# Denominators of the second attention layer: gathered into 32 rows per tile of tokens by four transfers, and one 128x4 product per block in place of four one-column products

## The chip, the cores and the metric

The kernel runs on one core of a Trainium2 chip. The metric is the device time of one execution in microseconds (us). Three runs of the kernel before the change took 3127.09, 3128.89 and 3130.44 us; the median is 3128.89 us.

## The reference, cut to what matters

Four images of 64x64 = 4096 tokens with 256 channels pass through two attention layers, one after the other. In each layer every token attends to all 4096 tokens of its image.

```
# layer 0
q, k, v = x @ Wq + bq, x @ Wk + bk, x @ Wv + bv        # 32, 32, 256 columns
x = gamma * softmax(q @ k.T) @ v + x
# layer 1
g, f, v = x @ Wg + bg, x @ Wf + bf, x @ Wh + bh        # 32, 32, 128 columns
x = x + softmax(g @ f.T) @ v @ Wo + bo
```

The softmax is computed without a maximum: the exponentials are summed unnormalised, the product with v is made from them, and the result is divided by the sum of the exponentials (the denominator) at the end. This case is about the denominators of layer 1.

## The kernel before, in words

**Blocks and steps.** An image takes 256 steps, 128 for each layer. In layer 1 the 4096 queries are cut into 8 blocks (j = 0 to 7) of 512, and a block takes 16 steps (i = 0 to 15), one for each 256 keys. A step makes the scores of 256 keys x 512 queries (L621, two steps ahead of their use), their exponentials p (L638, ScalarE), and the product of p with v (L713, TensorE). In the even steps ("split") p is cut into parts that TensorE multiplies faster: high (L631, ScalarE), low (L659) and d (L664, both VectorE). A block's accumulators are taken at step 15 (L770, L789) into o, 128 value columns x 512 queries.

**The sums.** The 16 tiles p of a block (128 partitions x 1024) have to be added up for the denominators. VectorE adds ten of them into p_sum (L678). The other six (steps 3, 5, 7, 9, 11 and 14; in the last image eight or seven) are added by transfers that accumulate into a tile p_sum_moved (L650 the first, L652 the others, here called moves). In images 0 to 2 all moves of a block go into one tile, so each waits until the one before has landed; in the last image they go into two tiles in turn, which a last transfer (L654) adds up. In the next block VectorE adds p_sum_moved to p_sum (add_moved, L778) and folds the two halves into the tile sums of 128 x 512 (fold, L782).

**The outputs.** `end_second` (L773) puts the rest of the work of a finished block into steps of the next block. `put(n, "a", ...)` runs it at the start of step n, and `put(n, "b", ...)` after the scores of that step were issued and before its products; "11b" below is the second place of step 11. For each of the four tiles t of 128 queries there are three stages: `multiply` (TensorE: o times Wo, L799, and then the column of denominators, L800: the 128x128 slice of sums as weights, a column of ones as the moving operand), `divide` (VectorE: reciprocal, L803) and `give` (ScalarE scales into y, L807, and a transfer adds y to the output in memory, L809). `multiply` stands at 9b, 10b, 12b and 13b of the next block (L67), at 5b to 8b in the kernel's last block (L68), and at 1b to 4b when the next block is the next image's first one of layer 0. The kernel's very last block is finished by code of its own (L836 to L875), which the change leaves as it is.

**What sets the order.** From step 8 on the order of instructions on each engine is the order in which the program issues them. Each engine works through its own list in that order and waits where an operand isn't there. All accumulating transfers are issued by POOL (GpSimd), together with the loads of q and k (L543) and, in layer 0, the residuals (L754, L1011). So a transfer that waits on POOL holds up every transfer behind it. When a sum on VectorE is issued is planned by two clocks (L1034, L1038, L1053) with a cost for each step, 0.63 us for each output among them.

**Buffers.** PSUM for side products (tag "side") has 2 buffers, shared by the outputs and the projections; the tiles "small" have 4; the tile p_sum_moved of images 0 to 2 and the tile sums have one each.

Of the kernel before, what the change touches and what calls it, by code (L numbers as in the profile page):

```python
# [50 lines left out]
F32 = mybir.dt.float32  # L51
F32R = mybir.dt.float32r
I32 = mybir.dt.int32
AF = mybir.ActivationFunctionType
ALU = mybir.AluOpType
AX = mybir.AxisListType

P = 128
QB = 512
QB0 = 256  # L60
NT = QB // P
S = 32
# [1 line left out]
EPS = 2.0**-12  # L64
UP = 2.0**12
AHEAD = 3
OUT_AT = (9, 10, 12, 13)  # L67
LAST_OUT_AT = (5, 6, 7, 8)  # L68
MOVED_AT = 1
KEEP, AHEAD_OF = 3, 1.0  # L70
Q_AHEAD = 6
# [179 lines left out]
def fast_path(ctx: ExitStack, tc: tile.TileContext, x, w0, w1, wo, bo, gamma, out, off):  # L251

    nc = tc.nc
    B, N, C = x.shape
# [8 lines left out]
    NI = (N // (G[0] * P), N // (G[1] * P))  # L263
# [8 lines left out]
    const = ctx.enter_context(tc.tile_pool(name="const", bufs=1))  # L272
    data = ctx.enter_context(tc.tile_pool(name="data", bufs=1))
    work = ctx.enter_context(tc.tile_pool(name="work", bufs=2))
    dram = ctx.enter_context(tc.tile_pool(name="dram", bufs=1, space=bass.MemoryType.DRAM))
# [25 lines left out]
    rows = {}  # L301
# [18 lines left out]
    nc.sync.dma_start(ident_dram, ident)  # L320
    ones = const.tile([P, 1], F32, name="ones")
    nc.vector.memset(ones, 1.0)

    inverse = const.tile([P, 2, B * N // P], F32, name="inverse")
    seen_v = const.tile([P, 2, B * NH], F32, name="seen_v")
# [29 lines left out]
    def side_psum(name):  # L355
        return ps_side.tile([P, QB], F32, tag="side", name=name)
# [3 lines left out]
    for j in range(NB):  # L360
        forms = {}
        for what, col in (("h", 1.0), ("l", 0.0), ("d", -EPS)):
            t = const.tile([P, NT, W], F32R, tag=f"v0{what}_{j}", name=f"v0{what}_{j}")
# [24 lines left out]
    q_t, moved_sums, first_p, later_sums, v_whole = {}, {}, [], [], {}  # L388
# [3 lines left out]
    def put(n, slot, *stages):  # L392
        todo.setdefault((n, slot), []).extend(stages)
# [167 lines left out]
    last_block = B * PER_IMAGE - NI[1]  # L561
# [30 lines left out]
    def small(name):  # L592
        return work.tile([P, C], F32, tag="small", bufs=4, name=name)
# [179 lines left out]
    def end_second(b, j, acc, p_sum, o, n_next):  # L773
        key = f"{b}_{j}"
        sums = [None]

        def add_moved():
            nc.vector.tensor_add(p_sum, p_sum, moved_sums[b, j, 0])  # L778

        def fold():  # L780
            sums[0] = work.tile([P, QB], F32, tag="sums", bufs=1, name=f"sums_{key}")
            nc.vector.tensor_add(sums[0].rearrange("p (a n) -> p a n", n=QB0), p_sum[:, :NS, :], p_sum[:, NS:, :])  # L782

        wait = j < NQ[1] - 1
        if not wait:
            while later_sums:
                later_sums.pop(0)[2]()
        for h in range(QB // QB0):
            nc.vector.tensor_add(o[h][:, :QB0], o[h][:, :QB0], acc[1][:, h * QB0 : (h + 1) * QB0])  # L789

        def output(t):
            tok = slice(t * P, (t + 1) * P)
            n = (b * N + j * QB) // P + t
            held = {}

            def multiply():
                held["ps"] = ps = side_psum(f"pso_{key}_{t}")
                part = o[t // NS][:, t % NS * P : (t % NS + 1) * P]
                nc.tensor.matmul(ps[:, :C], part, wo_sb, start=True, stop=True)  # L799
                nc.tensor.matmul(ps[:, C : C + 1], sums[0][:, tok], ones[:, :1], start=True, stop=True)  # L800

            def divide():
                nc.vector.reciprocal(inverse[:, 1, n : n + 1], held["ps"][:, C : C + 1])  # L803

            def give():
                y = small(f"y_{key}_{t}")
                nc.scalar.activation(y, held["ps"][:, :C], AF.Copy, scale=inverse[:, 1, n : n + 1])  # L807
                row = j * QB + t * P
                nc.gpsimd.dma_start(out[b, row : row + P, :], y, accum_op=ALU.add)  # L809

            return multiply, divide, give

        out_at = (1, 2, 3, 4) if not wait else OUT_AT if n_next < last_block else LAST_OUT_AT
        if wait:
            put(n_next + MOVED_AT, "b", lambda: later_sums.append((1.15, n_next + MOVED_AT + 3, add_moved, None)))
            put(n_next + MOVED_AT, "b", lambda: later_sums.append((0.6, n_next + MOVED_AT + 4, fold, f"p_sum_{b}_{j}")))
        else:
            put(n_next, "b", add_moved, fold)
        for t in range(NT):
            multiply, divide, give = output(t)  # L820
            at = n_next + out_at[t]
            put(at, "b", multiply)
            put(at + 1, "a", divide)
            put(at + 1, "b", give)

    ending = {}

# [64 lines left out]
    def put_all(n, at, stages):  # L892
        for where, stage in zip(at.split(), stages):
            put(n + int(where[:-1]), where[-1], stage)
# [64 lines left out]
    tensor_clock, vector_clock = 0.0, 0.0  # L959
# [27 lines left out]
    for n, s in enumerate(steps):  # L987
        now[0] = n
        b, l, j = s.b, s.l, s.j
# [24 lines left out]
        if ahead is not None and ahead.first:  # L1014
            k = (ahead.b, ahead.l, ahead.j * (QB0, QB)[ahead.l] // QB)
# [13 lines left out]
        if l == 0:  # L1029
            s.cut_both()  # L1030
            after.cut_low()
        else:
            cost = 1.9 if s.split else 2.2
            tensor_clock += cost + 1.7 * (b + 1 < B and s.i in (3, 7)) + 0.63 * (j > 0 and s.i in OUT_AT)  # L1034
            vector_clock = max(vector_clock, tensor_clock - cost)
            s.cut_both()
            after.cut_low()
            vector_clock += 1.15 * (s.split + after.split)  # L1038
            if n < len(steps) - 2:
                s.add_up(p_sum)  # L1040
        if l == 1:
# [11 lines left out]
            while later_sums and (later_sums[0][1] <= n or vector_clock + later_sums[0][0] <= tensor_clock + AHEAD_OF):  # L1053
                took, _, issue, _ = later_sums.pop(0)
# [12 lines left out]
            if n == len(steps) - 1:  # L1067
                last_outputs(acc, o)
            elif s.last:
                vector_clock += 0.8  # L1070
                end_second(b, j, acc, p_sum, o, n + 1)
# [23 lines left out]
def tile_two_attention_layers(tc: tile.TileContext, *args):  # L1095
    nc = tc.nc
    with tc.tile_pool(name="flag", bufs=1) as pool:
        off = pool.tile([1, 1], I32, name="off")
        fast_path(tc, *args, off)
        flag = nc.values_load(off[0:1, 0:1], min_val=0, max_val=4 * P, skip_runtime_bounds_check_because="a count")  # L1100
        with tc.If(flag < 1, preferred_fallthrough_block=False, label="in_range") as usual:
            pass
        with usual.Else():
            general_path(tc, *args)
# [40 lines left out]
```

## Time and profile before

| | us |
|---|---|
| median of three runs | 3128.89 |
| the profiled execution, its own time | 3129.13 |
| its span, first to last instruction | 3127.4 |
| TensorE (PE) busy | 3093.8 (99%) |
| VectorE (DVE) busy | 2732.4 (87%) |
| ScalarE (ACT) busy | 2203.5 (70%) |
| GpSimd (POOL) busy | 791.8 (25%) |
| L799, 248 matmuls with Wo, busy | 74.0 |
| L800, 248 one-column matmuls, busy | 34.4 |
| L803, 124 reciprocals, busy | 20.1 |

There are 31 blocks whose outputs go this way, so 124 outputs; each product in plain 32-bit floats is two matmuls with a weight load each, hence 248. The granted TensorE clock is 0.999 of full speed over the span. In the lines below, "L713 PE MATMUL acc<-p,v 128*128 128x512 f32 x4" is line, engine, operation, the tile written and those read, the shape, and how often; numbers in front are the start in us from the first instruction and the time until the end, and what stands in brackets is the idle time of the engine before it and what ended it. PE's ends are modelled and overlap the next start, so PE's pace is read from start to start.

### The profile page before, as it was taken

What the parts mean: (1) busy time and instruction counts of PE and PEld (TensorE: products, weight loads), DVE (VectorE), ACT (ScalarE), POOL (GpSimd) and SP (SyncE); (2) the same over time, 40 slices, a digit from 0 to 9 for tenths busy, and PEclk for the clock granted to TensorE, in tenths of its full rate; (3) what the DMA queues carried; (4) which work ended last, traced back from release to release, by engine and by line L of the source; (5) the groups of instructions that cost most, each with busy time, mean ns of one, the idle gap of its engine ahead of it and who ended that gap; (6) DMA issues with size and microseconds to landing.
All of it is one profiled execution on the core that took longest, in us unless ns stands there. A gap on an engine that the chain in (4) does not pass through costs nothing.

```text
span 3127.4 us, 55023 instructions
## 1 busy us (share of the span) xinstructions
PE 3093.8 (99%) x20052; PEld 2692.9 (86%) x20052; DVE 2732.4 (87%) x3328; ACT 2203.5 (70%) x2900; POOL 791.8 (25%) x1157
## 2 busy tenths in 40 slices
PE   8999999999999999999999999999999999999998
PEld 7999999666799999866679999986668999997665
DVE  6899889988888989998889988998888888888887
ACT  7767777777677777777767777677776666667775
POOL 4111113222411111422241111132234111123332
PEclk9999999999999999999999999999999999999999
DMA  4344455656644444656554444465565333337776
GB/s 124 75 89 89 84 96 115 127 115 118 125 85 84 93 89 87 128 121 118 117 110 92 84 89 90 88 133 115 115 128 97 63 70 72 60 76 158 154 154 140
DMA packets 441606, 325.86 MB, mean 104 GB/s; under 512 B 264466, under 2 KB 386196, under 8 KB 441332
## 3 DMA queue, kind: packets, MB, share of 16 engines
q0 software_dynamic: 112272, 196.49, 34.9%
q1 hardware_dynamic: 328148, 125.47, 16.8%
q8 instruction: 162, 2.65, 0.4%
q14 instruction: 112, 0.92, 0.1%
q10 hardware_dynamic: 912, 0.33, 0.1%
HBM read 128.45 MB, written 95.49 MB: 72 GB/s over the span
## 4 chain that ended last, share of the span: by engine, by line
PE 88%; DVE 3%; DMA 3%; issue 2%; ACT 2%; POOL 1%; SPq 0%; DVEq 0%; POOLq 0%; ACTq 0%
PE acc L689 23%; PE acc_pair L689 23%; PE acc L713 21%; PE st L621 14%; PE psv L497 4%; DMA p_sum_moved<-p 2%; PE psqk L446 2%; PE pso L799 1%; POOL k L543 1%; ACT p L638 0%; PE pso L800 0%; DVE d L664 0%; DVE low L659 0%; DVE p_sum L678 0%; ACT v0l L524 0%
## 5 line engine op out<-in xcount | busy, mean ns | idle before, releaser
L631 ACT ACTIVATE high<-st,down 128x1024 fp32r<-128x1024 f32 x651 | 728.2, 1119 | 686.9 <-PE st L621 609.1
L638 ACT ACTIVATE p<-st 128x1024 f32<-128x1024 f32 x1024 | 1028.9, 1021 | 20.3 <-DMA p_sum_moved<-p 9.3
L659 DVE TENSOR_TENSOR low<-p,high 128x1024 fp32r<-128x1024 f32 x565 | 690.7, 1223 | 144.4 <-ACT p L638 136.8
L664 DVE SCALAR_TENSOR_TENSOR d<-low,high 128x1024 fp32r<-128x1024 f32 x547 | 667.5, 1220 | 15.3 <-PE acc L713 0.7
L621 PE MATMUL st<-q,k 128*128 128x256 f32 (+1 forms) x3072 | 661.5, 323 | 0.6 <-DMA q<-qk_dram 0.5
L621 PEld LDWEIGHTS st<-q,k 128*128 128x128 f32 x3072 | 472.1, 189 | 57.5 <-issue 8.1
L713 PE MATMUL acc<-p,v 128*128 128x512 f32 (+1 forms) x1028 | 487.6, 596 | 0.8 <-DVE o L789 0.7
L689 PE MATMUL acc<-v0d,d 128*128 128x258 f32 x2048 | 336.5, 286 | 5.0 <-DVE d L664 4.7
L689 PE MATMUL acc<-v0h,high 128*128 128x258 f32 x2048 | 330.9, 284 | 1.2 <-ACT high L631 1.2
L689 PE MATMUL acc_pair<-v0l,low 128*128 128x256 f32 (+1 forms) x2048 | 329.9, 283 | 0.0
L689 PE MATMUL acc_pair<-v0h,high 128*128 128x258 f32 x2048 | 329.6, 283 | 0.0
L689 PE MATMUL acc<-v0l,low 128*128 128x256 f32 (+1 forms) x2048 | 328.1, 282 | 1.1 <-DVE low L659 0.8
L689 PE MATMUL acc_pair<-v0d,d 128*128 128x258 f32 x2048 | 328.8, 282 | 0.0
L754 POOL DMA_DIRECT2D out<-x x128 | 114.8, 897 | 839.3 <-DVE x L748 831.4
L713 PEld LDWEIGHTS acc<-p,v 128*128 128x128 f32 x1028 | 187.6, 189 | 143.1 <-issue 124.4
L678 DVE TENSOR_TENSOR p_sum<-p_sum,p 128x1024 f32<-128x1024 f32 x239 | 291.2, 1219 | 0.5
L689 PEld LDWEIGHTS acc<-v0d,d 128*128 128x128 f32 x2048 | 280.9, 189 | 7.8 <-DVE d L664 5.9
L689 PEld LDWEIGHTS acc<-v0h,high 128*128 128x128 f32 x2048 | 281.5, 189 | 3.0 <-ACT high L631 1.4
L689 PEld LDWEIGHTS acc<-v0l,low 128*128 128x128 f32 x2048 | 280.9, 189 | 2.6 <-DVE low L659 2.6
L689 PEld LDWEIGHTS acc_pair<-v0l,low 128*128 128x128 f32 x2048 | 282.4, 189 | 0.1
L689 PEld LDWEIGHTS acc_pair<-v0h,high 128*128 128x128 f32 x2048 | 281.9, 189 | 0.2 <-DVE o L733 0.2
L689 PEld LDWEIGHTS acc_pair<-v0d,d 128*128 128x128 f32 x2048 | 281.6, 189 | 0.0
(173 smaller groups left out, 4231.6 us busy)
## 6 DMA issues: line engine op xcount, KB each, us to landing
p_sum_moved<-p POOLq DMA_DIRECT2D x207, 512.0 KB, 5.0
x_res<-in_x SPq DMA_DIRECT2D x128, 128.0 KB, 3.2
qk_dram<-qk_parts SPq DMA_DIRECT2D x128, 128.0 KB, 2.2
x_res<-bias POOLq DMA_DIRECT2D x128, 128.0 KB, 4.1
out<-bias SPq DMA_DIRECT2D x128, 128.0 KB, 4.0
out<-x POOLq DMA_DIRECT2D x128, 128.0 KB, 3.1
q<-qk_dram POOLq DMA_DIRECT2D x252, 64.0 KB, 4.0
out<-y POOLq DMA_DIRECT2D x124, 128.0 KB, 3.5
```

Source lines behind the costliest of these rows:

```text
L446: nc.tensor.matmul(t["ps"], wqk[l][:, c, :], x_parts[key][n][:, c, :], start=(c == n == 0), stop=(c == NCC - 1 and n == 1),)
L497: nc.tensor.matmul(ps[:, n, :], xT[key][:, c, n * P : (n + 1) * P], wv[l][:, c, :], start=(c == 0), stop=(c == NCC - 1),)
L543: nc.gpsimd.dma_start(dst[n * D : (n + 1) * D, :], parts[h, which])
L621: nc.tensor.matmul(st[:, g, :], k_t[b, l, kt // NT][:, kt % NT * P : (kt % NT + 1) * P], q_t[b, l, j * n // QB][:, q0 : q0 + n], start=Tru ...
L631: nc.scalar.activation(self.high, s_flat, AF.Exp, bias=down)
L638: nc.scalar.activation(self.p, s_flat, AF.Exp)
L659: nc.vector.tensor_sub(self.low, self.p, self.high.bitcast(F32))
L664: nc.vector.scalar_tensor_tensor(self.d, self.low.bitcast(F32), -UP, self.high.bitcast(F32), ALU.mult, ALU.add)
L678: nc.vector.tensor_add(p_sum, other, self.p)
L689: nc.tensor.matmul(acc[2 * s + which][:, :width], p[:, g, s * P : (s + 1) * P], v0[self.i][v][:, g, :width], start=self.first and what != ...
L713: nc.tensor.matmul(acc[which].rearrange("p (a n) -> p a n", n=QB0)[:, cols, :], v_part[:, g, :], p[:, g * NS : (g + 1) * NS, :][:, cols, : ...
L754: nc.gpsimd.dma_start(out_rows(b, j, s), x_new, accum_op=ALU.add)
```

## The change

Before any output is multiplied, four transfers on POOL bring the tile sums into another shape. `fold_rows` adds its lower 64 partitions to its upper 64 inside SBUF. `store_rows` writes these 64 x 512 to memory. `gather(0)` reads the first 32 rows back into a tile rows of 128 x 128, whose partition is 32 t + r (t the tile of 128 queries, r the row); `gather(1)` adds the other 32 rows to it. Then one product, with rows as weights and a constant 128 x 4 matrix `quarters` (ones where the partition belongs to tile t) as moving operand, gives the denominators of all four tiles, as four columns in PSUM; it stands right behind the first output's product with Wo. One reciprocal of 128 x 4 replaces four of 128 x 1.

The places change too. The four transfers are put at 5a, 6b, 7b and 8b of the next block, or at 1a, 2a, 2b and 3b of the next image's first block. The outputs move to 11b, 12b, 14b and 15a, or 5a, 5b, 6b and 7a; the kernel's last block has no places of its own any more. The last dates for add_moved and fold are one step earlier, and the planner's cost for an output is 0.43 us at the last four steps. By the order of instructions of the changed kernel, POOL's list in a block of images 0 to 2 is: move of step 3, fold_rows, move of 5, store_rows, move of 7, gather(0), gather(1), move of 9, the four loads of q, move of 11, and so on; in the last image fold_rows stands behind the moves of 2 and 3, gather(0) ahead of the move of 8 and gather(1) behind it; in the kernel's last block gather(1) stands behind the L654 transfer.

```diff
-OUT_AT = (9, 10, 12, 13)
-LAST_OUT_AT = (5, 6, 7, 8)
+OUT_AT = "11b 12b 14b 15a"
+FIRST_OUT_AT = "5a 5b 6b 7a"
+GATHER_AT = "5a 6b 7b 8b"
+FIRST_GATHER_AT = "1a 2a 2b 3b"
...
+    quarters = const.tile([P, NT], F32, name="quarters")
+    nc.vector.memset(quarters, 0.0)
+    for t in range(NT):
+        nc.vector.memset(quarters[t * S : (t + 1) * S, t : t + 1], 1.0)
...
+        def fold_rows():
+            nc.gpsimd.dma_start(sums[0][: P // 2, :], sums[0][P // 2 :, :], accum_op=ALU.add)
+        def store_rows():
+            held["dram"] = dram.tile([P // 2, QB], F32, name=f"sums_dram_{key}")
+            nc.gpsimd.dma_start(held["dram"], sums[0][: P // 2, :])
+        def gather(k):
+            def issue():
+                if k == 0:
+                    held["rows"] = small(f"rows_{key}")[:, :P]
+                accumulate = dict(accum_op=ALU.add) if k else {}
+                part = held["dram"][k * S : (k + 1) * S, :].rearrange("r (t q) -> t r q", q=P)
+                nc.gpsimd.dma_start(held["rows"], part, **accumulate)
+            return issue
...
                 nc.tensor.matmul(ps[:, :C], part, wo_sb, start=True, stop=True)
-                nc.tensor.matmul(ps[:, C : C + 1], sums[0][:, tok], ones[:, :1], start=True, stop=True)
+                if t == 0:
+                    nc.tensor.matmul(ps[:, C : C + NT], held["rows"], quarters, start=True, stop=True)
             def divide():
-                nc.vector.reciprocal(inverse[:, 1, n : n + 1], held["ps"][:, C : C + 1])
+                if t == 0:
+                    nc.vector.reciprocal(inverse[:, 1, n : n + NT], held[t][:, C : C + NT])
...
-            put(n_next + MOVED_AT, "b", lambda: later_sums.append((1.15, n_next + MOVED_AT + 3, add_moved, None)))
-            put(n_next + MOVED_AT, "b", lambda: later_sums.append((0.6, n_next + MOVED_AT + 4, fold, f"p_sum_{b}_{j}")))
+            put(n_next + MOVED_AT, "b", lambda: later_sums.append((1.15, n_next + 3, add_moved, None)))
+            put(n_next + MOVED_AT, "b", lambda: later_sums.append((0.6, n_next + 4, fold, f"p_sum_{b}_{j}")))
...
+        put_all(n_next, gather_at, (fold_rows, store_rows, gather(0), gather(1)))
+        for t, at in enumerate(out_at.split()):
+            n, slot = n_next + int(at[:-1]), at[-1]
             multiply, divide, give = output(t)
+            put(n, slot, multiply)
+            if slot == "b":
+                put(n + 1, "a", divide)
+                put(n + 1, "b", give)
+            else:
+                put(n, "b", divide, give)
...
-            tensor_clock += cost + 1.7 * (b + 1 < B and s.i in (3, 7)) + 0.63 * (j > 0 and s.i in OUT_AT)
+            tensor_clock += cost + 1.7 * (b + 1 < B and s.i in (3, 7)) + 0.43 * (j > 0 and s.i >= NI[l] - NT)
```

## The prediction

> **What bounds the kernel now.** I read the page's busy times first, then its chain, then the waits of PE, and then timelines of one steady block and of the tail.
>
> ```profile
> PE 3093.8 (99%) x20052; PEld 2692.9 (86%) x20052; DVE 2732.4 (87%) x3328; ACT 2203.5 (70%) x2900; POOL 791.8 (25%) x1157
> ...
> PE 88%; DVE 3%; DMA 3%; issue 2%; ACT 2%; POOL 1%; SPq 0%; DVEq 0%; POOLq 0%; ACTq 0%
> ```
> ```profile
> PE pso L799 <- DVE v0d L533: 2.7, 3, 1.8
> ```
>
> PE is busy for 99% of the span; the waits of PE, summed over their view, are some 25 us, over half of them in the first 100 us. So what PE saves in layer 1 is saved from the time, and every wait that is put into PE's list is paid in full. The quoted wait is three stops of the outputs in the last blocks of images 0 to 2. Now PE around two outputs of a steady block (image 1, block 3; start, us until the end, what):
>
> ```profile
> 1432.53 0.59 PE L799 MATMUL pso<-wo,o 128*128 128x256 f32 x2
> 1432.96 0.28 PE L800 MATMUL pso<-ones,sums 128*128 128x1 f32 x2
> 1433.10 1.96 PE L713 MATMUL acc<-p,v 128*128 128x512 f32 x4
> 1434.50 1.03 PE L713 MATMUL acc<-v0h,v 128*128 128x512 f32 x2
> ...
> 1435.83 0.59 PE L799 MATMUL pso<-wo,o 128*128 128x256 f32 x2
> 1436.26 0.28 PE L800 MATMUL pso<-ones,sums 128*128 128x1 f32 x2
> ```
> ```profile
> 3114.97 1.05 PE L845 MATMUL ps_last<-ones,sums_last 128*128 128x1 f32 x8 [0.49 <-DVE sums_last L840]
> 3115.88 1.11 PE L713 MATMUL acc<-p,v 128*128 128x256 f32 x4
> ```
>
> Start to start, L799 takes 0.43 us and L800 0.14; the four matmuls of acc<-p that follow take 1.40, where they take 1.31 elsewhere (1564.83 to 1566.14), so L800 also costs 0.08 behind itself: 0.22. The second fence agrees: eight one-column matmuls in a row start 0.91/8 = 0.114 us apart, so two cost 0.225. Last, POOL in the next block (image 1, block 4) and at the end:
>
> ```profile
> 1457.43 0.56 POOL L650 DMA_DIRECT2D p_sum_moved<-p  x1 [7.79 <-ACT p L638]
> 1462.06 0.87 POOL L652 DMA_DIRECT2D p_sum_moved<-p  x1 [4.07 <-ACT p L638]
> 1467.08 0.87 POOL L652 DMA_DIRECT2D p_sum_moved<-p  x1 [4.15 <-ACT p L638]
> 1473.12 0.86 POOL L652 DMA_DIRECT2D p_sum_moved<-p  x1 [5.18 <-ACT p L638]
> 1473.66 2.34 POOL L543 DMA_DIRECT2D q<-qk_dram  x4
> ```
> ```profile
> 3099.99 0.87 POOL L652 DMA_DIRECT2D p_sum_moved<-p  x1 [1.18 <-DMA p_sum_moved<-p]
> 3106.64 0.87 POOL L654 DMA_DIRECT2D p_sum_moved<-p_sum_moved  x1 [5.79 <-DMA p_sum_moved<-p]
> 3107.18 2.13 POOL L809 DMA_DIRECT2D out<-y  x2
> ```
> ```profile
> x_res<-bias POOLq DMA_DIRECT2D x128, 128.0 KB, 4.1
> ...
> out<-y POOLq DMA_DIRECT2D x124, 128.0 KB, 3.5
> ```
>
> The moves of steps 3, 5, 7 and 9 follow one another at the pace of landings, not of p: they land at 1461.53, 1466.56 and 1472.59, and the next starts 0.52 to 0.53 later each time (p of step 5 was ready at 1457.2). And the queue lands in order: the first load of q, issued 0.54 behind a move, lands 0.26 behind it; a y behind a move 0.7 behind it. The moves are a chain that nobody waits for now. The change hangs PE's list on that chain.
>
> **Part by part.**
>
> *Removed.* 124 one-column products go and 31 four-column ones come. Width doesn't price them: 128-column matmuls (L497) also start 0.111 us apart. So 93 x 0.225 = 20.9 us of PE go; the three of the kernel's last block are in the tail's sum, leaving 90 x 0.225 = 20.3. The three stops of L799 (2.7) go too: the outputs stand at 11b and later, behind the projections of 9b. Together **23.0 us**. The 93 reciprocals (161 ns each, 15 us of DVE) and five memsets at the start are worth nothing: DVE is no bound, and PE covers it.
>
> *The last wait in steady blocks.* The fourth transfer can't be issued before the third has landed; the third stands behind the move of step 7 in POOL's list; and PE's four-column product at 11b waits for the fourth. In block 4 of image 1, on the clock of before: the first move is held by add_moved on DVE (ends 1456.86, the move starts 0.57 later). add_moved itself comes 0.82 later, because two of the old block's outputs (2 x 0.43) now stand at 14b and 15a, between this block's first scores and the p that DVE waits for. So the first move is at 1458.25, the move of 7 lands 15.16 later as before, at 1473.41, gather(0) 0.35 behind it at 1473.76, and POOL issues gather(1) 0.53 later, at 1474.29. PE is at 11b at 1476.38 now (10b plus 2.06); minus two whole outputs that leave 9b and 10b (2 x 0.65), plus the 0.86, plus its own product with Wo (0.43): 1476.37. So PE waits for whatever gather(1) takes **beyond 2.08 us**. The same working over blocks 1 to 5 of images 0 to 2 gives 2.28 us on average over these 15; blocks 6 have 1.4 us more and don't wait.
>
> gather(1) isn't in the trace: 64 KB, memory to SBUF, accumulating, 128 pieces of 512 B. From below, plain loads of q and k of 64 KB land 1.9 to 2.1 us after issue when alone. From above, x_res<-bias, the one row that accumulates from memory into SBUF (128 KB), has a median of 4.05 (least 3.60). Between them lies y, 128 pieces, accumulating, 3.1 when alone. I take 3.1, for the pieces and the adding. That is 0.82 x 15 = **12.3 us** (0 to 26.6).
>
> [...]
>
> *The other blocks.* In blocks 7 of images 0 to 2 the loads of k stand in between; the same working gives 0.2, 0.3 and 1.5: **2.0** (0 to 5). At the three changes of image nothing stands between: from the end of fold (1614.86 in image 1) a lone y's 3.1, a store's 2.2 (qk_dram), a lone load's 2.0, the 3.1 and four starts of 0.53 make 12.5 us. PE's 4b is at 1627.50; plus that output (0.65) and the products behind it (0.96), less four outputs that leave (2.6), plus Wo (0.43), it is at 5a at 1626.94, 12.1 after fold: 0.4 each, **1.3** (0 to 4).
>
> *The last image, blocks 1 to 6.* Here POOL itself stops: fold_rows stands ahead of the move of 5 and waits for fold, which ends at 2949.6 in block 3 where that move was issued at 2948.14. fold_rows starts at 2950.1, the move of 5 at 2950.7, that of 6 lands behind it near 2957.8, store_rows at 2958.2, gather(0), started 0.53 later, at 2960.8; gather(1), issued at 2961.3 behind the move of 8 (which lands near 2964), lands at 2964.6. PE is there at 2962.9 (10b at 2960.88, plus 2.06, the shifts cancel): 1.7 x 6 = **10.2 us** (0 if the move of 6 lands as it does now, at 2955.5; 16 with the dear gather).
>
> *The tail.* gather(1) stands behind the L654 transfer, as the two y do now: issued at 3107.18, the first y lands 0.7 behind L654, at 3112.3. PE is at 11b at 3105.19 now; without the four outputs of 5b to 8b (2.6) and a stop of 0.41, and with Wo's 0.43, at 3102.6. It waits 9.7 us. Behind that stand 0.22, the 9.3 that PE now needs from 3105.19 to the first half of its last product (3114.48), and three outputs (1.29): the last denominators start at 3123.1 and not at 3114.97, **8.1 us** later (up to 9.2). Nothing hides it: PE's list has the product at that place, and the work behind it can't go ahead.
>
> *What hides the rest.* POOL gets 124 more transfers of 0.5 to 0.9 us; it is busy a quarter of the time. q lands some 2 us later, with 3 us to spare before 14b. The moves of 9 and 11 land 1 to 3 us later, so buffers of p come free later; ACT waits for that 9.3 us in all now, and its p is made about a step ahead. I take nothing; without that cover it is 0.5 us a block.
>
> **Sum.** -23.0 + 12.3 + 2.0 + 1.3 + 10.2 + 8.1 = +10.9. The profiled execution took 3129.13 (span 3127.4 and 1.7 around it), 0.24 above the median: 3129.1 + 10.9 = **3140 us**.
>
> **The rivals.**
> - *The rows come in time.* gather(1) takes 2.2 us or less and the last image's chain doesn't slip. Then the 23.0 stand against the tail's 8.1: 3129.1 - 14.9 = **3114**, with half of the last image's wait 3119. For it: the plain loads, and the 2.28 us that are there. Against it: both accumulating rows. It turns faster where the mean wait at 11b falls under about 0.2 us a block.
> - *The moves slip too.* If gather(1) costs 4.05 as x_res does, the bounds above add to 26.6 + 5 + 4 + 16 + 9.2 = 61, so 3129.1 + 38 = **3167**; p's buffers, freed late, add to it at 0.5 us a block. For it: each move waits for the landing before it, so one late start passes down the block. Against it: ACT is idle 30%.
> - *The one-column products were covered anyway*, so that nothing is saved. Against it: PE's starts follow without a gap. It ends with the rival before, and I count it there.
>
> **Chances.** 0.2% is about what a measurement of this kernel can tell from no change: 6.3 us. Forecast 0.54 (3131 to 3152), of which 0.13 lies within 0.2%. Rows in time 0.26, of which 0.19 is faster and 0.07 within. Slip 0.20, slower. So faster 0.19, same 0.20, slower 0.61. The range goes from the sum with the unknowns at their low ends, 3114, to nearly that at their high ends, 3164.
>
> **What would show it.** PE's waits should have a new first row, the product with quarters waiting for the gathers' DMA, some 25 stops of about 1 us and one of nearly 10 at the end; L800's place should show 62 matmuls. gather(1)'s row in the DMA issues decides the 15 blocks: 3.1 as forecast, 2.2 for the first rival, 4 for the second. If ACT's waits for p_sum_moved grow past 20 us, the moves slip. I am wrong if PE reaches 11b later than I count, for then the rows are in time, or if the transfers don't land in the order of issue.

## The result, and the profile after

The changed kernel takes **3279.47 us** (median of 6 runs, 3275.49 to 3290.22), the kernel before 3129.71 us beside it (6 runs, 3127.09 to 3132.60). The ratio is 1.0486, 95% interval 1.0468 to 1.0504: 4.9% slower. The forecast was 3140 us with a range up to 3164, so the sign was right and the size far off. The profiled execution took 3290.22 us, its span is 3288.4 us (before: 3127.4).

The page's busy times and its chain, by engine:

```profile
PE 3141.8 (96%) x19866; PEld 2704.3 (82%) x19866; DVE 2729.4 (83%) x3240; ACT 2201.0 (67%) x2900; POOL 897.8 (27%) x1281
...
PE 73%; issue 10%; DMA 8%; POOL 4%; ACT 3%; DVE 2%; SPq 0%; POOLq 0%; DVEq 0%; ACTq 0%
```

Two things are new. PE has 186 matmuls less and yet is busy 48 us longer. And the chain, which was 88% PE, now runs through DMA, POOL and "issue". The waits of PE (engine, tile, line, what it waited for: us in total, times, longest):

```profile
PE pso L825 <- DMA rows<-sums_dram: 110.6, 31, 10.0
PE acc L695 <- DVE d L670: 5.9, 7, 1.3
...
PE pso L823 <- ACT y L833: 3.4, 3, 1.2
```

The first line is the product with `quarters`: it stops PE once in each of the 31 blocks, 3.6 us on average. L823 is the product with Wo (L799 before); its three stops are at the changes of image. POOL and PE in image 1, block 4, the block that the prediction worked through (start, us, engine, line, operation; in brackets the idle time before it):

```profile
1522.86 0.89 POOL L658 DMA_DIRECT2D p_sum_moved<-p  x1 [3.82 <-ACT p L644]
1523.47 1.00 POOL L812 DMA_DIRECT2D rows<-sums_dram  x1
1529.66 1.12 POOL L812 DMA_DIRECT2D rows<-sums_dram  x1 [5.19 <-DMA rows<-sums_dram]
1530.38 1.33 POOL L658 DMA_DIRECT2D p_sum_moved<-p  x1
```
```profile
1530.56 0.59 PE L823 MATMUL pso<-wo,o 128*128 128x256 f32 x2
1534.39 0.59 PE L825 MATMUL pso<-quarters,rows 128*128 128x4 f32 x2 [3.23 <-DMA rows<-sums_dram]
1534.84 3.76 PE L719 MATMUL acc<-p,v 128*128 128x512 f32 x4
```

The order is as predicted: move of 7, gather(0), gather(1), move of 9. By the trace the move of 7 lands at 1527.92, gather(0) at 1528.69, and gather(1), issued at 1529.66, at 1534.35; PE goes on 0.04 us later. The last line shows what no term of the prediction had: the next product starts 2.77 us after this one (1537.61), where the same four matmuls took 1.31 to 1.40 before. The stretches around it say why (us, busy PE, PEclk = granted TensorE clock, DMA share, GB/s):

```profile
1527.00:1534.02 7.02, 4.16 (x16) 1.00 0.33 54
1534.02:1540.84 6.82, 6.45 (x13) 0.50 0.63 121
1540.84:1548.00 7.16, 7.16 (x28) 1.00 0.71 110
```

For 6.82 us around the end of the stop PE is granted **half its clock**. After the first 100 us the trace has 28 such periods, nearly all of 3.41 or 6.83 us, 165.8 us together (the last begins behind PE's last product); PE was idle in 35.7 us of them, so they cost (165.8 - 35.7) / 2 = 65 us. In the kernel before there is one, in the last 6 us.

### The profile page after: what moved, and what is told of

Its sections match the earlier page's. It is cut to its first block, busy times and chain, and to the rows that moved or that the text cites. A ratio compares the mean times of both kernels' runs of the same rounds, so it can differ in the third digit from the quotient of the medians.

```text
span 3288.4 us, 54839 instructions
## 1 busy us (share of the span) xinstructions
PE 3141.8 (96%) x19866; PEld 2704.3 (82%) x19866; DVE 2729.4 (83%) x3240; ACT 2201.0 (67%) x2900; POOL 897.8 (27%) x1281
## 3 DMA queue, kind: packets, MB, share of 16 engines
q0 software_dynamic: 135088, 208.83, 35.8%
## 4 chain that ended last, share of the span: by engine, by line
PE 73%; issue 10%; DMA 8%; POOL 4%; ACT 3%; DVE 2%; SPq 0%; POOLq 0%; DVEq 0%; ACTq 0%
PE acc L695 21%; PE acc_pair L695 21%; PE acc L719 14%; PE st L627 11%; DMA rows<-sums_dram 5%; PE psv L503 3%; DMA p_sum_moved<-p 2%; PE psqk L452 2%; ACT p L644 2%; POOL p_sum_moved L658 1%; PE pso L823 1%; POOL rows L812 1%; POOL k L549 1%; PE pso L825 0%; POOL out L835 0%
## 5 line engine op out<-in xcount | busy, mean ns | idle before, releaser
L644 ACT ACTIVATE p<-st 128x1024 f32<-128x1024 f32 x1024 | 1025.6, 1021 | 35.8 <-PE st L627 17.5
L627 PE MATMUL st<-q,k 128*128 128x256 f32 (+1 forms) x3072 | 673.0, 327 | 1.1 <-DMA q<-qk_dram 0.5
L719 PE MATMUL acc<-p,v 128*128 128x512 f32 (+1 forms) x1028 | 524.3, 635 | 0.5 <-DVE o L795 0.4
L719 PEld LDWEIGHTS acc<-p,v 128*128 128x128 f32 x1028 | 202.3, 201 | 153.3 <-issue 134.2
```

The source lines that it names most:

```text
L627: nc.tensor.matmul(st[:, g, :], k_t[b, l, kt // NT][:, kt % NT * P : (kt % NT + 1) * P], q_t[b, l, j * n // QB][:, q0 : q0 + n], start=Tru ...
L644: nc.scalar.activation(self.p, s_flat, AF.Exp)
L719: nc.tensor.matmul(acc[which].rearrange("p (a n) -> p a n", n=QB0)[:, cols, :], v_part[:, g, :], p[:, g * NS : (g + 1) * NS, :][:, cols, : ...
```

## The experiments

The theory after the result: PE loses the stops themselves (110.6 us) and the half clock that they bring on (some 65 us); the saving of the prediction is there, underneath. The rivals: the lower clock stands beside the stops for some other reason; or the transfers cost time even where PE doesn't wait for them.

| run | us, median | ratio to before, 95% |
|---|---|---|
| changed kernel | 3279.5 | 1.0468 to 1.0504 |
| product's operands always there | 3182.8 | 1.0157 to 1.0191 |
| the same, second gather overwrites | 3137.6 | 1.0015 to 1.0037 |
| the same, no transfers | 3115.9 | 0.9939 to 0.9970 |
| stops filled with PE work | 3248.5 | 1.0372 to 1.0407 |
| second gather overwrites | 3211.7 | 1.0247 to 1.0281 |
| two plain gathers, two products | 3130.4 | 0.9995 to 1.0014 |
| before, 93 columns left out | 3112.8 | 0.9932 to 0.9959 |
| outputs later | 3221.5 | 1.0280 to 1.0311 |
| last block the old way | 3276.7 | 1.0438 to 1.0476 |
| halves added by VectorE, 12b 13b | 3162.5 | 1.0090 to 1.0121 |
| halves added by VectorE, 12b 13a | 3126.4 | 0.9978 to 0.9996 |
| the same, last block the old way | 3122.9 | 0.9971 to 0.9992 |

### Is it only PE's wait? The product's operands always there

```diff
-nc.tensor.matmul(ps[:, C : C + NT], held["rows"], quarters, start=True, stop=True)
+nc.tensor.matmul(ps[:, C : C + NT], wo_sb[:, :P], quarters, start=True, stop=True)
...
-nc.vector.reciprocal(inverse[:, 1, n : n + NT], held[t][:, C : C + NT])
+nc.vector.reciprocal(inverse[:, 1, n : n + NT], quarters)   # filled with ones
```

> The four transfers run as in the changed kernel, but the four-column product takes a part of Wo as weights, which is always there, and the reciprocal reads a constant: the denominators are left out of the output. Theory: all of the loss is the 31 stops of PE (110.6 us in the profile after) and the half clock that follows them (clock 0.975 over the span, some 80 us at half speed lost); without them what the change saves is left, 3129.7 - 23 = 3107, range 3103 to 3114, clock 0.998 or more. Rival: the transfers themselves, the moves that start later and the shifted outputs cost time too; then the time stays above 3120 though PE never waits for rows, and ACT or DVE show the new waits.

Measured: 3182.8 us, neither of the theory's 3107 nor the changed kernel's 3279. The stops are gone, but others came, as the rival had it. From the waits of PE and of ACT (first ACT's in the kernel before), and POOL's timeline in image 1, block 4:

```profile
PE st L627 <- DMA q<-qk_dram: 25.5, 17, 4.6
```
```profile
ACT p L638 <- DMA p_sum_moved<-p: 9.3, 7, 2.7
```
```profile
ACT p L644 <- DMA p_sum_moved<-p: 54.4, 34, 5.7
```
```profile
1476.54 0.89 POOL L658 DMA_DIRECT2D p_sum_moved<-p  x1 [3.80 <-ACT p L644]
1477.14 1.00 POOL L812 DMA_DIRECT2D rows<-sums_dram  x1
1483.76 1.12 POOL L812 DMA_DIRECT2D rows<-sums_dram  x1 [5.62 <-DMA rows<-sums_dram]
1484.48 1.33 POOL L658 DMA_DIRECT2D p_sum_moved<-p  x1
```

ACT waits for buffers of p that moves still hold, and PE for q, which is loaded behind them. POOL sits 5.62 us between the two gathers; the move of 9 is issued 2.49 us after the landing of the move of 7 (1481.99) and not 0.53, and takes 7.30 us to land (5.0 is the median of a move). From this block's first move to that of the next POOL takes 40.5 us (1466.34 to 1506.84); before, a steady block takes 38.5. So the theory that the stops are all was wrong: right beneath them lies a second bound, the chain of moves.

### The same, with the second gather overwriting, and with no transfers

```diff
-accumulate = dict(accum_op=ALU.add) if k else {}
+accumulate = {}
```
```diff
-put_all(n_next, gather_at, (fold_rows, store_rows, gather(0), gather(1)))
```

> The run in which the four-column product always has its operands (3182.8; denominators left out), with the second gather writing over the first instead of adding: it still waits for the first gather's landing and holds POOL until then. It splits the 67 us that the four transfers cost without any wait of PE for rows (3182.8 - 3115.9 without them). Theory (the adding lengthens the chain of moves: the move behind it took 7.3 us and not 5): the block gets 2 us shorter in the 21 blocks that it bounds and in the last image, 3130 to 3145. Rival (POOL's wait for the first gather is the price): 3165 to 3183.

> As the run in which the four-column product always has its operands (denominators left out), and the four transfers are not issued at all. Theory 2 (the transfers hold up POOL's moves, and these p's buffers and the loads of q): the 53 us that the run with the transfers lost go, 3129.6 - 16 to -23 = 3107 to 3116. Rival (the outputs' new places, 11b to 15a, and PE's shifted list cost that much by themselves): 3150 to 3185.

Measured: 3137.6 and 3115.9 us, both as the theory had them. POOL with the overwriting gather, image 1, block 4:

```profile
1474.92 0.71 POOL L812 DMA_DIRECT2D rows<-sums_dram  x1 [4.48 <-DMA rows<-sums_dram]
1475.61 1.01 POOL L658 DMA_DIRECT2D p_sum_moved<-p  x1
```

By the trace this gather lands in 3.11 us and the move behind it in 5.59. Over all blocks the medians are 4.61 us with adding and 3.16 without, and 7.12 against 5.65 for the move behind it. So of the 67 us that the transfers cost without any wait of PE for rows, 45 are the adding and 22 the rest. Some 19 of the 67 lie in blocks 1 to 5 of images 0 to 2 (39.0 us each on average from first scores to first scores, 37.7 without transfers), 22 in blocks 1 to 6 of image 3 (37.8 and 34.2). Without transfers little else is lost (the run below that only leaves the removed products out takes 3112.8 us): the outputs' new places are harmless, and the page reads

```profile
PE 3075.4 (99%) x19866; PEld 2677.2 (86%) x19866; DVE 2728.8 (88%) x3240; ACT 2198.6 (71%) x2900; POOL 788.8 (25%) x1157
```

This run issues the same 19866 matmuls as the changed kernel, and gives the account of its loss: the spans differ by 3288.4 - 3113.9 = 174.5 us; the stops are 110.6, PE's busy time is 3141.8 - 3075.4 = 66.4 longer, and -2.5 is left over. Worked out from its periods, half clock costs 65 us in the changed kernel and 4.9 in this run, so it is 60 of the 66.4; what the other 6 are isn't shown.

### Does the stop bring on the half clock? The stops filled

```diff
+for _ in range(1 + 8 * (t == 0)):
     nc.tensor.matmul(ps[:, :C], part, wo_sb, start=True, stop=True)
```

> The changed kernel with the first output's product with Wo made nine times instead of once, ahead of the four-column product; the output is the same. Eight repeats of 0.43 us are 3.4 us of PE work that stands where PE now waits (15 steady stops of 3.5 us on average). Theory (the stop also costs the clock): the wait is merely filled, it can't end earlier, and where a stop was shorter than 3.4 us the filling adds the rest, about 15 us over all blocks; but PE is not idle, the half-clock windows go except around the 10 us stop at the end, and about 70 us with them: 3279 - 70 + 15 = 3224, range 3205 to 3245, clock over 0.99. Rival (the stops alone are the loss, the lower clock is beside them or has another cause): 3279 + 15, 3285 to 3300, clock still 0.975.

Measured: 3248.5 us. PE does 31 x 3.44 = 106.6 us of useless work more and the kernel is 31 us *faster*. Page and waits:

```profile
PE 3184.8 (98%) x20362; PEld 2767.2 (85%) x20362; DVE 2728.2 (84%) x3240; ACT 2199.0 (68%) x2900; POOL 895.6 (28%) x1281
```
```profile
PE pso L826 <- DMA rows<-sums_dram: 21.6, 15, 9.0
```

The granted clock is 0.998 over the span (0.975 in the changed kernel). The rival, 3285 to 3300, is out: the clock falls because PE stands still. The theory's 3224 was 24 us too low (its range ended at 3245), partly because it went by the profiled execution of the changed kernel, which lies 11 us above the median of its runs, partly because stops of 21.6 us stay, 9.0 of them in the last block with half clock behind it. By spans, the run without transfers plus the repeats plus these stops gives 3113.9 + 106.6 + 21.6 = 3242; 3245.7 was measured.

How long must a stop be? In five profiles (changed kernel and the first four runs, first and last 100 us left out), PE stops by their length, and how many have a half-clock period beginning during them or up to 3.5 us behind: 0.7 to 1.3 us 0 of 60; 1.3 to 2 us 9 of 33; 2 to 2.75 us 3 of 8; longer 30 of 30 (the changed kernel alone: 0 of 7, 2 of 5, 3 of 5, 20 of 20). In the eight other runs it is 23 of 24 of the longer ones: one of 2.92 us (outputs later) had no half clock behind it.

What decides is not the length alone. The half-clock periods of a run all begin on one grid of 3.413 us, to 0.002 us. If the time of all 14 profiles (first 100 and last 60 us left out) is cut into windows by that grid and PE's idle time is added up in each, then of the windows at full clock with over 2 us of idle time all 65 were followed by one at half clock, of those with 1.6 to 2 us 14 of 35, of those with less 0 of 12,133 (the changed kernel alone: 24 of 24, 2 of 4, 0 of 845). The stop of 2.92 us lay across an edge, 1.36 us before and 1.56 behind. A window at half clock was followed by another one in 33 of 34 cases with over 0.5 us of idle time, and in 0 of 73 with under 0.2. (PE's ends are modelled, so these bounds are too.)

### What makes the rows late? Overwriting, and two plain halves

The second gather overwrites, PE waits for it (the diff of above, on the changed kernel):

> The second gather writes over the first instead of adding to it, so half of the rows are left out of the denominators; its place in the queue, its 128 pieces and its bytes are the same. Theory (adding, memory into SBUF, is what made it 4.6 us and not the 1.9 to 2.2 us of the plain loads): it lands in 2 to 2.8 us, each of the 31 stops shrinks by about 2 us (-60) and most of the half-clock windows of the blocks with stops near 3.5 us go (-40 to -60): 3160 to 3185. Rival (the pieces or the place in the queue make its price): it still takes over 4 us, 3265 to 3285.

Measured: 3211.7 us, between the two ranges. Its gather lands in 3.15 us (median), not in 2 to 2.8: adding is 1.5 us of the 4.64, and the plain transfer in this place is a good 3 us and not 2. The stops shrink less than expected,

```profile
PE pso L825 <- DMA rows<-sums_dram: 65.3, 29, 9.4
```

by 45.3 us, and the clock rises to 0.990; PE's busy time falls by 33.7 us, so 1.5 us off each stop are worth 68 us.

Two plain gathers into the halves of one tile, and two products that add them up:

```diff
-GATHER_AT = "5a 6b 7b 8b"
+GATHER_AT = "5a 6b 7b 7b"
...
-nc.gpsimd.dma_start(held["rows"], part, **accumulate)
+nc.gpsimd.dma_start(held["rows"][:, k * P : (k + 1) * P], part)
...
+for k in (0, 1):
+    nc.tensor.matmul(ps[:, C : C + NT], held["rows"][:, k * P : (k + 1) * P], quarters,
+                     start=k == 0, stop=k == 1)
```

> The two gathers are plain and go into the two halves of one small tile, the second issued right behind the first (7b), and two four-column products into the same columns add them up. This undoes one part of the change, the second gather's wait for the first and its adding. Theory: the rows are there 0.5 to 1 us after the first gather, which landed at 1528.69 where PE arrived at 1531.2, so the steady stops go, those of the last image shrink to about 1 us, and the stop in the last block goes since no gather is behind the L654 transfer: 3129.7 - 23 + 31 x 0.11 + up to 8 of stops left = 3110 to 3120, clock over 0.995. Rival (the first gather, behind a move, is itself late, or the transfers cost elsewhere): stops of over 1 us stay in the steady blocks, 3140 to 3200.

Measured: 3130.4 us, no different from before, and outside both ranges. All 149 us between this run and the changed kernel hang on the second gather's adding and its wait for the first:

```profile
PE pso L825 <- DMA rows<-sums_dram: 6.3, 7, 3.6
```

By the trace, in image 1, block 4, the gathers land at 1473.12 and 1473.30, and the move of 9 starts 0.55 after the landing of the move of 7. The steady block takes 37.95 us from first scores to first scores, 38.48 before. The expected 3110 to 3120 was missed because the second product is two matmuls, 0.22 us and not 0.11 (6.9 in all), the stop in the last block stayed (3.6), and the three stops on ACT's y (3.4) replaced those of L799.

### What is the removed work worth? 93 columns left out of the kernel before

```diff
+if t == 0:
     nc.tensor.matmul(ps[:, C : C + 1], sums[0][:, tok], ones[:, :1], start=True, stop=True)
```

> The kernel before with 93 of its 124 one-column products left out (the first tile's denominators of a block are copied for the other three by VectorE, so the denominators of three tiles of four are left out); nothing else changes. It prices the work that the change removes. By the starts of PE that the prediction used, 0.225 us each: 3129.6 - 20.9 = 3108.7. By the sum of PE's busy times in the later runs (3184.8 with eight repeats of 0.43 us in 31 blocks, 3078.2 without them, against 3093.8 before), 0.168 each: 3114. Rival (they were covered): 3125 or more.

Measured: 3112.8 us, 17.4 less than before. The steady block takes 37.81 us and not 38.48: 0.67 for three products, 0.223 each, which is the price that the prediction read from PE's starts. Not all of it reaches the end: the three stops of L799 are 3.6 us (2.7 before), and the last block isn't shorter.

### Can the outputs wait? Places and the last block

```diff
-OUT_AT = "11b 12b 14b 15a"
+OUT_AT = "13a 13b 14b 15a"
```

> The changed kernel with the outputs at 13a 13b 14b 15a and not 11b 12b 14b 15a: the product that needs the rows stands a step and a half later, 3.6 us in images 0 to 2 and 3.3 us in image 3. Theory 1 (stops and the half clock behind them are all): of the steady stops some 3 us in all stay, of image 3 some 9, of the tail 6.7, of the image changes 4.9, with 8 to 10 of half clock: 3129.6 - 16 + 24 + 9 = 3147, range 3140 to 3155. Theory 2 (formed on the run with the product that always had its operands, 3182.8): the four transfers lengthen POOL's chain of moves, 36.4 us from the first move to the last landing and 40.3 us from block to block there, where the kernel before had 38.5, so that the chain bounds the block when PE no longer waits for rows: 3182.8 + 5 to 15 for the tail and the changes of image = 3185 to 3200, with waits for q and for p_sum_moved in place of the stops.

Measured: 3221.5 us, outside both. PE's waits:

```profile
PE pso L823 <- ACT y L833: 39.2, 38, 2.6
PE pso L825 <- DMA rows<-sums_dram: 26.1, 16, 7.4
```

The 38 stops are the experiment's own: at these places a product with Wo takes the PSUM buffer of an output whose y ACT has just been given. Less these, 3182 is left. That is the time of the run that never waits for rows, but 26.1 us of waits for rows are still in it, so the agreement proves nothing. ACT waits 55.1 us for p_sum_moved as it did there (54.4). That speaks for the chain of moves as the second bound, but the run by itself doesn't show it.

The kernel's last block the old way (`old = n_next >= last_block`: one-column products at 5b to 8b, no transfers):

> The changed kernel, but in the kernel's last block the denominators are made as before: one-column products at 5b to 8b, no transfers. It prices the tail alone. The prediction's 8.1 us, and half of the 6.8 us that the half clock behind that stop costs: 3279.5 - 11 = 3268, range 3262 to 3273. Rival (the end is set by something else in the changed kernel, such as the moves of the last block): within 4 us of 3279.

Measured: 3276.7 us (3266.2 to 3283.8), outside the expected range and inside the rival's. By the times alone this can't be told from the changed kernel. By the traces it can: from the last block's first scores to the end it takes 51.7 us before, 63.8 in the changed kernel and 52.2 here. The tail is worth 11.6 us; the 30 other stops, 103.4 us here and 100.6 there, took some of it back.

VectorE adds the two halves, so that one product is left, with two sets of places:

```diff
+nc.vector.tensor_add(held["rows"][:, :P], held["rows"][:, :P], held["rows"][:, P:])   # at 11b
...
-OUT_AT = "11b 12b 14b 15a"
+OUT_AT = "12b 13b 14b 15a"     # second run: "12b 13a 14b 15a"
```

> Two plain gathers into the halves of one tile as in the run before (3130.4), but VectorE adds the halves (11b, or 4a at a change of image) and one four-column product is left; the outputs stand at 12b 13b 14b 15a and at 4b 5a 6a 7a. Expected from that run's profile: -6.9 for 31 products of 0.22 us, -3.6 for the stop in the last block, -3.4 for the three stops on ACT's y at the changes of image: 3116, range 3111 to 3122, which would be faster than the kernel before. Rival (VectorE stands in its list until the rows are there, and low and d of the next steps behind it come late): 3125 to 3145, with PE waiting for d or low in the steady blocks.

> Two plain gathers into the halves of one tile, VectorE adds them (11b, or 4b at a change of image), one four-column product; outputs at 12b 13a 14b 15a, so that no product with Wo takes the buffer of a y given just before it, which cost 28 stops of 1.1 us in the run with 12b 13b 14b 15a (3162.5); at the changes of image the places are those of the changed kernel. Theory: 3130.4 of the run with two products, less 6.2 (31 products at 0.2) and 2 to 3 of the stop in the last block: 3121, range 3116 to 3126, faster than the kernel before. Rival (the reciprocal and y now wait for VectorE's add): stops on DVE rows or ACT y of 0.5 us or more per block, 3130 to 3150.

Measured: 3162.5 us, a miss, for the same reason as above:

```profile
PE pso L825 <- ACT y L835: 33.7, 28, 1.7
```

The second output at 13a in place of 13b gives its buffer back half a step earlier, these stops go, and the time is 3126.4 us, just above the expected range (at the changes of image this run has the changed kernel's places again). The rival, stops on VectorE's add, was 2.2 us in all. With the last block the old way as well:

> The run with plain gathers into two halves that VectorE adds (3126.4), and in the kernel's last block the denominators are made as before, without transfers. In that run's profile the last block took 57.0 us from its first scores to the end, in the kernel before 51.7, and with the old way in the last block of the changed kernel 52.2: 3126.4 - 4.8 + 0.7 for three one-column products = 3122, range 3117 to 3126, which is faster than the kernel before by 0.2 to 0.3%. Rival (the last block's end is set by the moves, which stay): 3126 or more.

Measured: 3122.9 us, ratio 0.9981 (0.9971 to 0.9992): this version is 0.2% faster than the kernel before.

```profile
PE 3076.7 (99%) x19872; PEld 2674.9 (86%) x19872; DVE 2733.7 (88%) x3273; ACT 2202.0 (71%) x2900; POOL 875.3 (28%) x1277
```

Of the 17 us that PE no longer works, some 7 arrive at the end. The first steady blocks take 37.7 us as they do without transfers; the blocks of image 3 take 34.7 to 35.8 (34.2 without transfers), where PE waits for q, which is still behind the moves.

## Why the prediction was wrong

**Where PE waits: right.** One stop per block at the product with `quarters`, behind gather(1), behind gather(0), behind the move of 7. Nothing of it was missing. That the stop in the last block was right in size (9.7 predicted, 10.0 measured) is luck. I had the L654 transfer land 8.9 us behind PE's arrival and gather(1) 0.7 behind that. In the changed kernel this transfer (L660) lands at 3259.68, 7.5 behind, and gather(1) at 3262.18, 2.5 behind that:

```profile
3255.07 0.86 POOL L660 DMA_DIRECT2D p_sum_moved<-p_sum_moved  x1 [4.65 <-DMA p_sum_moved<-p]
3255.63 1.46 POOL L812 DMA_DIRECT2D rows<-sums_dram  x1
```
```profile
3262.22 0.59 PE L825 MATMUL pso<-quarters,rows 128*128 128x4 f32 x2 [9.99 <-DMA rows<-sums_dram]
```

**How long it waits in steady blocks: mis-sized.** The step that failed is "I take 3.1, for the pieces and the adding", with 4.05 as the upper end. The prediction's chain had gather(0) landing 0.35 us behind the move, POOL going on 0.53 later, and 3.1 for gather(1). Measured over blocks 1 to 6 of images 0 to 2 (means): 0.93, 0.72 and 4.59, so 2.3 us later. 0.82 predicted plus 2.3 is 3.1; 3.5 was measured: 52.8 us for the 15 blocks and not 12.3. The price lay outside both rows that bounded it: 3.1 turned out to be that of the transfer *without* adding (3.15), and x_res, the only accumulating row from memory into SBUF, should have been the nearest row and not the upper end.

**The other blocks: mis-sized too.** Blocks 6 0 predicted against 6.4 measured, blocks 7 2.0 against 8.3, the changes of image 1.3 against 4.9, image 3 10.2 against 28.4. The stops sum to 110.6 us where the prediction had some 35.

**How much the price is worth.** The run whose second gather overwrites has about the price that I took, 3.15 us, and still takes 3211.7 us. So the price is 68 of the 139 us by which the forecast was off. The other 72 are there without it: the stops are 65.3 us where the sum had 33.9 (25.9 and not 12.3 in the 15 steady blocks, 19.4 and not 10.2 in image 3), PE is busy 32.7 us longer than without transfers, and some 9 us less are saved.

**What a stop costs: missing.** The sum added the stops as if each cost its length. PE's half clock behind them costs another 60 to 66 us, 2 us a stop. The trace of before could not show it, since behind the first 100 us PE's longest stop there is 1.8 us; no rival had it. In the tail 11.6 us were measured where I had 8.1; a period of 13.65 us at half clock, 7.88 of it idle, is 2.9 of that.

**What hides the rest: wrong in general, unpunished here.** "I take nothing; without that cover it is 0.5 us a block." Without PE's stops the moves' delay costs 67 us, over 2 us a block. In the changed kernel PE is so late that ACT seldom notices (11.8 us of waits for p_sum_moved ahead of p, 9.3 before). With a second gather of 3.15 us it is still hidden (13.0 us); it comes out where PE doesn't wait for rows.

**What is saved: right per product, too high in sum.** 0.223 us each against 0.225; of 20.9 us 17.4 arrive. The three stops of L799 (2.7) went as predicted, but three others on ACT's y at the changes of image (3.4) came, which I had put at nothing. 14.2 us remain in the run without transfers and waits for rows, where I had 23.0.

**The rival "the moves slip too"** (3167) named the price, 4.05 and up, but not what it does to the clock. With the measured stops and PE's longer busy time the sum is 3113.9 + 110.6 + 66.4 = 3290.9 against a span of 3288.4.

## What to carry to other kernels

Price a transfer by the row that has its direction *and* its adding (the gather took 4.64 us with adding and 3.15 without), and let two gathers that don't need each other go side by side into two halves; one behind the other and adding, they made the kernel 149 us slower than side by side. A stop of the otherwise full TensorE cost its length here (110.6 us in 31 stops) and, where over 1.6 to 2 us of it fell into one window of 3.413 us, half clock behind it (53 of 54 stops of over 2.75 us): 60 to 66 us in all, 2 us a stop. One or two such windows at half clock lose an estimated 1.7 to 3.4 us, half their length. Before an operand of the bounding engine is hung behind a queue, follow that queue through a whole block: what holds up the queue may become the bound even where the operand is in time.

## What the runs showed of the hardware

Adding from memory into SBUF made a 64 KB transfer of 128 pieces take 4.64 us and not 3.15 (medians of the changed kernel and of the run whose second gather overwrites), and the 512 KB move right behind it in the queue 7.12 and not 5.65 (the two runs whose product always has its operands). In all 14 profiles a PE that idled over 2 us of a window of 3.413 us was granted half its clock in the next window (65 of 65); under 1.6 us it never was (0 of 12,133). Giving the idle PE useless products kept the clock at 0.998, where it was 0.975, and made the kernel 31 us faster.
